# Layer 3's first keys and values, made in layer 2: a change to a four-layer Perceiver kernel

## The chip, the cores and the metric

The kernel runs on one core of a Trainium2 chip. The time is the device time of one execution in microseconds (us). TensorE (PE) multiplies, VectorE (DVE) and ScalarE (ACT) work on its results in PSUM, GpSimd (POOL) works in SBUF, and SyncE (SP) issues most DMAs. Each engine runs its own list of instructions strictly in the order in which the compiler put them.

## The reference, cut to what matters

Four layers run one after the other on `x`, 2 batches of 256 rows of 256 numbers, each with a cross-attention, a self-attention and a feed-forward part. Here only the end of layer 2 and the cross-attention of layer 3 matter:

```
x = x + L2_xattn(ctx, layernorm(x))           # a long convolution; the last stage before the change
x = x + L2_attn(layernorm(x), Wq, Wk, Wv)     # 16 heads of 16, rotary positions
x = x + L2_ffn(layernorm(x), ...)             # an attention again, then 8 experts, 2 per row
x = x + L3_xattn(layernorm(x), ctx, ctx, w_q, w_kv, w_concat)

def _L3_xattn_ref(q, kv, mem, w_q, w_kv, w_concat):
    c = concatenate([mem, kv], axis=1)        # the context twice: the softmax is that over it once
    qh = heads(q @ w_q)                       # 16 heads of 16
    kvp = c @ w_kv                            # ONE head of keys and values, shared by all 16
    k, v = kvp[..., :16], kvp[..., 16:]
    return concat(softmax(qh @ k.T / 4) @ v) @ w_concat
```

The context `ctx` is an input, 2 batches of 4096 rows. So the keys and values of layer 3 depend on no earlier layer: they can be made whenever the context is in SBUF.

## The kernel before, in words

All is float32. `perceiver` (L2466) calls one function per stage; `banks` gives out the 8 PSUM banks anew for each group of stages: in layer 2 (stage set "c") 3 banks "mm", 3 "tr", 2 "acc", in layer 3's cross-attention 4 "mm" and 4 "tr". SBUF is taken in pools that are stacked on one another; a pool that lies where an older one lay can be written only when the older one has been given free.

**Order.** Inside a block `in_order(...)` (L338) the instructions of the named engines stay as the code lists them. Elsewhere a planner in the compiler orders each engine's instructions: it goes through the program with its own estimates of time and gives a free engine the earliest listed instruction that it believes ready. Later instructions can so be put into an earlier gap, and once the order is made the engine keeps it.

**Layer 2, `l2_attn` (L1651) and the first half of `l2_ffn` (L1666).** Both project q, k and v (in `l2_attn` with a rotation in between, `rope_heads` L692, whose table `rope` is loaded by SP at L697) and call `self_attention` (L757). That runs steps k = 0 to 23 in order. `maxima(k)`, for k < 16, multiplies queries with keys (L785, into two "mm" banks) and DVE takes the row maximum of each bank (L791). `weights(k - 6)`, from k = 6 on, makes the scores again the other way round (L801, "tr" banks) and ACT takes the exponential (L808). `shift` (L815, L817) and `weigh` (L826) come in between. In k = 0 to 5, the *first maxima*, there are no weights, and the "tr" banks lie unused. Between the two attentions, at the *border*, lie the sum with `x` (L1661) and a norm (L386), both on DVE and ACT.

**Layer 3, `l3_xattn` (L2049).** `ctx_chunks` (L461) loads a batch's context in four chunks of 1 MB. `keys(b)` (L2068) makes a list of 12 steps of a batch: 8 times `key` (two matmuls of 512 columns, an ACT copy with bias, L2079), and two times `value` (8 matmuls 32 columns wide, L2088, ACT L2093) and `turned` (4 transposes L2098, ACT L2099). The queries are normed and projected (`proj_heads`). Then, in one block in order: two `key` steps of batch 0; a *ramp* of 18 turns, each with four matmuls for maxima (L2126), four DVE maxima (L2130) and one step of the list `made`; and a main loop of 8 groups of 16 turns, with the maxima of the next group, the weights (L2154, ACT L2158) and the sums (L2170) of this one, and a step of `made` while any is left. Of the 24 steps of both batches 2 stand ahead of the ramp, 18 in it, and 4 in the first turns of the main loop:

```
made.pop(0)()
made.pop(0)()
made += keys(1)
steps = maxima()
for _ in range(18):
    next(steps)
    next(steps)
    if made:
        made.pop(0)()
```

Weights that all stages load go through one ring of 4 buffers (`weight`, L314), issued by SP.

Of the kernel before, what the change touches and what calls it, by code (L numbers as in the profile page):

```python
# [268 lines left out]
class Perceiver:  # L269
# [486 lines left out]

    def self_attention(self, pool, qT, kT, v, scale):  # L757

# [8 lines left out]
        with ExitStack() as s:  # L767
# [65 lines left out]
            with self.in_order(e.PE, e.DVE, e.Activation):  # L833
                for k in range(16 + 6 + 2):
                    its = []
                    if k < 16:
                        its.append(maxima(k))
                    if 0 <= k - 6 < 16:
                        its.append(weights(k - 6))
                    then = None  # L840
                    if its:
                        self.steps_in_turn(*its)
                    if k % 4 == 0 and 4 <= k <= 16:
                        shift(k // 4 - 1)()
# [821 lines left out]
    def l2_ffn(self, x):  # L1666
        nc = self.nc
        T = NT * P
        with ExitStack() as s:
            keep = s.enter_context(self.tc.tile_pool(name="l2f_keep", bufs=1))  # L1670
# [77 lines left out]
            def unit(j):  # L1748
                def front():
                    gu, down = self.of_expert(pool, experts, j, ("l2f_gu", 1), ("l2f_down", 1))  # L1750
                    hT = p3.tile([P, KC, P], F32, name="rowsT", tag="rowsT")
                    if j < straight:
                        self.turn_chosen(pool, hT, h2, ats, along, j, "norm2")
                    else:
                        self.turn_rows(hT, rows, j, "norm2")
                    return expert(gu, down, hT, P, "e"), down
# [46 lines left out]
    def sort_rows(self, pool, chosen, n):  # L1803
# [52 lines left out]
    def send_rows(self, pool, x, slots, xs, first, n):  # L1856
# [3 lines left out]
        for t in range(NT):  # L1860
            for slot in slots:
# [7 lines left out]
                sent.append(i.ins.name)  # L1869
        rows = pool.tile([P, n, D], F32, name="rows")  # L1870
        for a, b in ((first, first + 2), (first + 2, n)):
            i = nc.gpsimd.dma_start(rows[:, a:b, :], xs[a * P : b * P].rearrange("(j p) d -> p j d", p=P))
            for name in sent:
# [43 lines left out]
    def ways_back(self, pool, ats, down, weights, first, n):  # L1917
# [5 lines left out]
        for j in range(first, n):  # L1923
# [123 lines left out]


    def l3_xattn(self, x, cpool):  # L2049

# [9 lines left out]
        with ExitStack() as s:  # L2060
            pool = s.enter_context(self.tc.tile_pool(name="l3x", bufs=1))
            kp = s.enter_context(self.tc.tile_pool(name="l3x_k", bufs=2))
            pt_pool = s.enter_context(self.tc.tile_pool(name="l3x_pt", bufs=16))
            wk, wv, wq = self.weight("l3x_wk"), self.weight("l3x_wv"), self.weight("l3x_wq")
            PAIRS = ((0, 1), (2, 3))
            kv = {}

            def keys(b):  # L2068

                cT = self.ctx_chunks(cpool, b, bufs=4)  # L2070
                kT = kp.tile([P, NK], F32, name="kT", tag="kT")
                v = kp.tile([P, 2, 4, 4, 32], F32, name="v", tag="v")
                kv[b] = kT, v.rearrange("p u g i d -> p (u g i) d")
                vTs = {}

                def key(j):
                    ps = self.bank([P, 512], "tr")
                    self.mm(ps, [(wk[:, k, :], cT[j // 2][:, k, ts(j % 2, 512)]) for k in range(KC)])
                    nc.scalar.activation(kT[:, ts(j, 512)], ps, AF.Identity, bias=self.col("lead"))  # L2079

                def value(u):


                    ps = self.bank([P, 512], "tr")
                    for k in range(KC):
                        for g in range(4):
                            j = 4 * u + g
                            nc.tensor.matmul(  # L2088
                                ps[ts(g, 32)], wv[:, k, :], cT[j // 2][:, k, ts(j % 2, 512)],
                                start=k == 0, stop=k == KC - 1,  # L2090
                            )
                    vTs[u] = pool.tile([P, 512], F32, name="vT", tag="vT")
                    nc.scalar.activation(vTs[u], ps, AF.Identity, bias=self.col("behind"))  # L2093

                def turned(u):
                    ps = self.bank([P, 4, P], "tr")
                    for i in range(4):
                        nc.tensor.transpose(ps[:, i, :], vTs[u][:, ts(i, P)], self.ident)  # L2098
                    nc.scalar.copy(  # L2099
                        v[:, u].rearrange("p g i d -> p i g d"), ps.rearrange("p i (g d) -> p i g d", d=32)  # L2100
                    )

                return [partial(key, j) for j in range(8)] + [partial(f, u) for u in range(2) for f in (value, turned)]

            made = keys(0)
            xnT = self.to_T(self.layernorm(x))
# [32 lines left out]
            def shifted(t, half, pad):  # L2139
                ps = self.bank([P, 2, P], "tr")  # L2140
                for c in range(2):
                    nc.tensor.transpose(ps[:, c, :], pad[:, c, :], self.ident)
                ready[t, half] = kp.tile([P, 2, P], F32, name="qm", tag="qm")
                nc.vector.tensor_add(ready[t, half], ps, qT[:, ts(half, 2), ts(t, P)])
# [227 lines left out]
    def l3_ffn(self, x):  # L2372
        nc = self.nc
        with self.tc.tile_pool(name="l3f", bufs=1) as pool, self.tc.tile_pool(name="l3f3", bufs=3) as p3:
# [34 lines left out]
            def unit(j):  # L2409
                def front():  # L2410
# [6 lines left out]
                    else:  # L2417
                        self.turn_rows(rT, rows, j)
                    hT = p3.tile([P, 8, P], F32, name="hT", tag="hT")
# [46 lines left out]
def perceiver(tc, dram, out, col_at, row_at, layers=LAYERS):  # L2466
    with ExitStack() as ctx:
        k = Perceiver(ctx, tc, dram, col_at, row_at)
        x = k.xp.tile([P, NT, D], F32, name="xres", tag="xres")
        tc.nc.sync.dma_start(x, dram["x"])  # L2470
        banks, tern, conv = ExitStack(), ExitStack(), ExitStack()
        k.tern = tern.enter_context(tc.tile_pool(name="l0f_w", bufs=1))
        for name in layers:
# [17 lines left out]
            elif name == "l2_attn":  # L2491
                conv.close()
                banks.close()
                k.banks(banks, "c", 3, 3, 2)
            elif name == "l3_xattn":

                banks.close()
                k.banks(banks, "l3x", 4, 4, 0)
            elif name == "l3_attn":
                banks.close()  # L2500
                k.banks(banks, "b", 3, 3, 2)
# [34 lines left out]
```

## Time and profile before

| | us |
|---|---|
| three runs | 2663.58, 2667.24, 2675.09 (median 2667.24) |
| profiled execution | 2663.32 |
| its span, first to last instruction | 2661.6 |
| end of the convolution stage, start of `l2_attn` | about 1630.3 |
| first maxima of `l2_attn` | 1656.2 to 1666.3 |
| border between the two attentions | 1706.6 to 1712.5 |
| first maxima of `l2_ffn` | 1734.0 to 1744 |
| context chunks of batch 0 issued | 1932.5 |
| ramp of layer 3 | 1949.7 to 2010.3 |
| main loop of layer 3 | from 2010.3 |

The page's first part gives the busy time of each engine and its share of the span. The second cuts the span into 40 equal slices of 66.5 us; each digit is a busy share in tenths, and the row PEclk is the share of its full clock that TensorE was granted. The timeline lists instructions in order of time: start, duration, engine, line, operation, result and operands, how many were merged (x4), and in brackets how long the engine had been idle and what ended that. One float32 matmul is two records of MATMUL in it, so x4 is two matmuls. Windows give, for stretches of time, the busy time of engines and the granted clock.

### The profile page before, as it was taken

What the parts mean: (1) busy time and instruction counts of PE and PEld (TensorE: products, weight loads), DVE (VectorE), ACT (ScalarE), POOL (GpSimd) and SP (SyncE); (2) the same over time, 40 slices, a digit from 0 to 9 for tenths busy, and PEclk for the clock granted to TensorE, in tenths of its full rate; (3) what the DMA queues carried; (4) which work ended last, traced back from release to release, by engine and by line L of the source; (5) the groups of instructions that cost most, each with busy time, mean ns of one, the idle gap of its engine ahead of it and who ended that gap; (6) DMA issues with size and microseconds to landing.
All of it is one profiled execution on the core that took longest, in us unless ns stands there. A gap on an engine that the chain in (4) does not pass through costs nothing. (4 is left out here: it accounts for less than half of the span.)

```text
span 2661.6 us, 45615 instructions
## 1 busy us (share of the span) xinstructions
PE 2493.7 (94%) x17709; PEld 1665.8 (63%) x17709; DVE 1727.2 (65%) x3195; ACT 1346.4 (51%) x2545; POOL 915.1 (34%) x861
## 2 busy tenths in 40 slices
PE   8986999999999999999799998889989999999889
PEld 6853566666666666666433555557835666554678
DVE  5566577777777777777669655454267788754542
ACT  3323666666666666666466322331116777784522
POOL 0520255655655655656459313001101222110010
PEclk9987999999999999999899998889999999999789
DMA  7210322222242222222300100017530000003656
GB/s 256 83 56 23 115 72 64 66 71 64 66 126 72 68 69 64 71 67 80 111 16 1 64 20 24 1 48 262 194 135 17 2 2 2 2 2 113 222 210 218
DMA packets 77111, 214.11 MB, mean 80 GB/s; under 512 B 6392, under 2 KB 21312, under 8 KB 66400
## 3 DMA queue, kind: packets, MB, share of 16 engines
q1 hardware_dynamic: 72128, 202.69, 22.9%
q0 software_dynamic: 1888, 5.90, 0.7%
q8 instruction: 139, 2.28, 0.4%
q10 hardware_dynamic: 2880, 2.62, 0.3%
q14 instruction: 76, 0.62, 0.1%
HBM read 190.48 MB, written 20.71 MB: 79 GB/s over the span
## 5 line engine op out<-in xcount | busy, mean ns | idle before, releaser
L1059 POOL TENSOR_TENSOR total<-total,S 128x512 f32<-128x512 f32 x434 | 542.2, 1280 | 304.7 <-ACT S L1048 304.7
L1048 ACT ACTIVATE S<-S 128x512 f32<-128x512 f32 x512 | 302.0, 625 | 209.5 <-DVE S L1045 209.3
L2130 DVE TENSOR_REDUCE mx<-ps_mm 128x1 f32<-128x512 f32 x512 | 318.0, 684 | 75.6 <-PE ps_tr L2154 58.9
L1034 DVE TENSOR_TENSOR most<-ps_mm,most 128x512 f32<-128x512 f32 x448 | 278.3, 684 | 119.2 <-ACT S L1031 119.2
L1031 ACT COPY S<-ps_mm 128x512 f32<-128x512 f32 x512 | 263.0, 599 | 116.7 <-PE ps_mm L1024 115.4
L1045 DVE TENSOR_TENSOR S<-S,ps_dec 128x512 f32<-128x512 f32 x512 | 317.6, 680 | 0.2 <-PE ps_dec L1103 0.2
L2158 ACT ACTIVATE PT<-ps_tr 128x512 f32<-128x512 f32 x476 | 246.9, 602 | 93.9 <-PE ps_tr L2154 89.0
L358 PEld LDWEIGHTS ps_tr<-w_l1x_wv,ctxT 128*128 128x128 f32 x2048 | 246.9, 192 | 52.9 <-issue 52.6
L1071 PE MATMUL acc<-S,v 128*64 128x256 f32 x2048 | 250.7, 387 | 7.8 <-ACT v L335 5.1
L1024 PE MATMUL ps_mm<-qT,kT 64*128 64x256 f32 x2048 | 257.1, 391 | 0.0
L358 PE MATMUL ps_tr<-ctxT,w_l1x_wk 128*128 128x512 f32 x512 | 251.8, 615 | 0.0
L2126 PE MATMUL ps_mm<-kT,qT 32*128 32x512 f32 x1024 | 250.6, 621 | 0.2 <-DVE mx L2130 0.2
L358 PE MATMUL ps_tr<-w_l1x_wv,ctxT 128*128 128x128 f32 x2048 | 250.1, 275 | 0.0
L2154 PE MATMUL ps_tr<-qm,kT 32*128 32x256 f32 x1904 | 239.7, 390 | 0.0
L1024 PEld LDWEIGHTS ps_mm<-qT,kT 64*128 64x128 f32 x2048 | 188.3, 187 | 38.9 <-DVE most L1034 3.8
L1071 PEld LDWEIGHTS acc<-S,v 128*64 128x64 f32 x2048 | 136.3, 137 | 104.8 <-ACT S L1031 38.8
L2154 PEld LDWEIGHTS ps_tr<-qm,kT 32*128 32x128 f32 x1904 | 170.3, 185 | 17.0 <-issue 6.5
L2179 POOL TENSOR_TENSOR sums<-sums,part 128x256 f32<-128x256 f32 x102 | 73.7, 722 | 269.2 <-ACT part L2178 269.2
L358 PEld LDWEIGHTS ps_tr<-ctxT,w_l1x_wk 128*128 128x128 f32 x512 | 89.7, 190 | 101.4 <-issue 99.9
L335 DVE COPY v<-ps_tr 128x512 f32<-128x512 f32 x120 | 82.9, 691 | 89.0 <-PE ps_tr L358 88.9
L2170 PE MATMUL ps_tr<-PT,v 128*32 128x256 f32 x2048 | 139.6, 385 | 0.0
L2126 PEld LDWEIGHTS ps_mm<-kT,qT 32*128 32x128 f32 x1024 | 85.5, 185 | 60.7 <-issue 48.4
(544 smaller groups left out, 3832.8 us busy)
## 6 DMA issues: line engine op xcount, KB each, us to landing
ctxT<-in_ctxT SPq DMA_DIRECT2D x144, 512.0 KB, 3.6
ctxT<-in_ctxT SPq DMA_DIRECT2D x16, 1024.0 KB, 7.5
w_l2f_gu<-in_l2f_gu SPq DMA_DIRECT2D x16, 1024.0 KB, 6.5
bd_dram<-bd SPq DMA_DIRECT2D x8, 1536.0 KB, 6.0
w_l3f_w<-in_l3f_w SPq DMA_DIRECT2D x11, 1028.0 KB, 8.2
w_l3f_w<-in_l3f_w SPq DMA_DIRECT2D x11, 1024.0 KB, 5.2
ctx<-in_ctx SPq DMA_DIRECT2D x8, 1024.0 KB, 4.9
w_l2f_down<-in_l2f_down SPq DMA_DIRECT2D x16, 512.0 KB, 4.1
```

The lines of the kernel that those rows point to most:

```text
L358: self.nc.tensor.matmul(out, lhsT, rhs, start=i == 0, stop=i == len(pairs) - 1)
L1024: nc.tensor.matmul(banks[hh, i][:, j, :], k[part, ts(2 * i + j, P)], q[u][part, :], start=True, stop=True)
L1031: nc.scalar.copy(t, ps)
L1034: nc.vector.tensor_tensor(m, ps, m, ALU.max)
L1045: nc.vector.tensor_tensor(t, t, spread[u][:, hh, :].unsqueeze(1).to_broadcast([P, 2, L]), ALU.add)
L1048: nc.scalar.activation(t, t, AF.Exp)
L1059: nc.gpsimd.tensor_add(tot, tot, t)
L1071: nc.tensor.matmul(av[u][part], vs[:, 2 * i + j, part], got[hh, i][:, j, :], start=g % 8 == 0 and i + j == 0, stop=g % 8 == 7 and i + j == 2,)
L2126: nc.tensor.matmul(ps, qT[rows, 2 * half + c, ts(t, P)], kT[rows, ts(j, 512)], start=True, stop=True,)
L2130: nc.vector.tensor_reduce(mx[:, c, r, j : j + 1], ps, AX.X, ALU.max)
L2154: nc.tensor.matmul(ps[:, i, :], kT[rows, ts(2 * u + i, P)], q[rows], start=True, stop=True)
L2158: nc.scalar.activation(pt, ps, AF.Exp, scale=0.25)
```

## The change

A function `l3_open`, called before `l2_attn`, opens a pool for keys, values and weights that lives through layer 3, and a pool for batch 0's context that lives until layer 2's second attention is done. It loads the two weights and the four context chunks and makes the 12 steps of batch 0. Four of them (`key` 0 to 3) run in `l2_attn`'s attention, one after each of the maxima k = 1 to 4; five (`key` 4 to 7, `value` 0) are listed at the border, outside any block in order; three (`turned` 0, `value` 1, `turned` 1) run after the maxima k = 1 to 3 of `l2_ffn`'s attention. In layer 3 only batch 1's 12 steps are left; they go into the first 12 turns of the ramp, and batch 1's chunks are loaded where batch 0's were. To make room, `sort_rows` uses the constant `ones`, `send_rows` keeps only the row tiles that are read from it, `other` shares two buffers with `places`, `qm` and `x1` move to other pools, and `l3x_wk`, `l3x_wv` leave the ring of weights.

```diff
-    def self_attention(self, pool, qT, kT, v, scale):
+    def self_attention(self, pool, qT, kT, v, scale, beside=()):
...
                     if its:
                         self.steps_in_turn(*its)
+                    if 0 < k <= len(beside):
+                        beside[k - 1]()
                     if k % 4 == 0 and 4 <= k <= 16:
...
-            z = self.self_attention(pool, qT, kT, v, 0.25)
+            z = self.self_attention(pool, qT, kT, v, 0.25, self.early[:4])
+            del self.early[:4]
             y = self.xp.tile([P, NT, D], F32, name="xres", tag="xres")
+            for step in self.early[:5]:
+                step()
+            del self.early[:5]
             for t in range(NT):
                 self.nc.vector.tensor_add(y[:, t, :], z[:, t, :], x[:, t, :])
...
-                z = self.self_attention(pool, qT, kT, v, 0.25)
+                z = self.self_attention(pool, qT, kT, v, 0.25, self.early)
                 zT = self.to_T(z, pool, "zT")
-                x1 = self.linear(zT, self.weight("l2f_wo"), x0, out=keep.tile([P, NT, D], F32, name="x1"))
+                x1 = self.linear(zT, self.weight("l2f_wo"), x0, out=self.kv.tile([P, NT, D], F32, name="x1"))
+            self.early_ctx.close()
...
-        before, ones = f("before", P), f("ones", P)
+        before, ones = f("before", P), self.ones
-        nc.gpsimd.memset(ones, 1.0)
...
-        rows = pool.tile([P, n, D], F32, name="rows")
+        rows = pool.tile([P, n - first, D], F32, name="rows")
...
-            other = pool.tile([P, NT * P], F32, name="other", tag="other")
+            other = pool.tile([P, NT * P], F32, name="other", tag="places", bufs=2)
...
+    def l3_open(self, ctx):
+        self.kv = ctx.enter_context(self.tc.tile_pool(name="l3x_kv", bufs=1))
+        self.l3w = []
+        for name in ("l3x_wk", "l3x_wv"):
+            self.l3w.append(self.kv.tile(list(self.dram[name].shape), F32, name=name))
+            self.nc.sync.dma_start(self.l3w[-1], self.dram[name])
+        self.early_ctx = ExitStack()
+        pool = self.early_ctx.enter_context(self.tc.tile_pool(name="l3x_ctx", bufs=1))
+        self.kv_first, self.early = self.l3_keys(self.kv, pool, self.ctx_chunks(pool, 0, bufs=4))
+
+    def l3_keys(self, kp, pool, cT):
...
+        kT = kp.tile([P, NK], F32, name="kT")
+        v = kp.tile([P, 2, 4, 4, 32], F32, name="v")
+        vTs = {}
+
+        def key(j):
+            ps = self.bank([P, 512], "tr")
+            self.mm(ps, [(wk[:, k, :], cT[j // 2][:, k, ts(j % 2, 512)]) for k in range(KC)])
+            nc.scalar.activation(kT[:, ts(j, 512)], ps, AF.Identity, bias=self.col("lead"))
+
+        def value(u):
...
+            vTs[u] = pool.tile([P, 512], F32, name="vT", tag="vT")
+            nc.scalar.activation(vTs[u], ps, AF.Identity, bias=self.col("behind"))
+
+        def turned(u):
...
+        steps = [partial(key, j) for j in range(8)] + [partial(f, u) for u in range(2) for f in (value, turned)]
+        return (kT, v.rearrange("p u g i d -> p (u g i) d")), steps
...
-            kv = {}
+            kv = {0: self.kv_first}
...
-            made = keys(0)
+            made = keys(1)
...
             with self.in_order(mybir.EngineType.PE, mybir.EngineType.DVE, mybir.EngineType.Activation):
-
-                made.pop(0)()
-                made.pop(0)()
-                made += keys(1)
                 steps = maxima()
...
                 k.banks(banks, "c", 3, 3, 2)
+                k.l3_open(first)
```

More of the change, by code (lines that the diff above doesn't have):

```diff
@@ L1669, in l2_ffn @@
         with ExitStack() as s:
-            keep = s.enter_context(self.tc.tile_pool(name="l2f_keep", bufs=1))
             with self.tc.tile_pool(name="l2f", bufs=1) as pool:
@@ L1754, in front @@
                     else:
-                        self.turn_rows(hT, rows, j, "norm2")
+                        self.turn_rows(hT, rows, j - straight, "norm2")
                     return expert(gu, down, hT, P, "e"), down
@@ L1869, in send_rows @@
                 sent.append(i.ins.name)
-        rows = pool.tile([P, n, D], F32, name="rows")
+        rows = pool.tile([P, n - first, D], F32, name="rows")
         for a, b in ((first, first + 2), (first + 2, n)):
-            i = nc.gpsimd.dma_start(rows[:, a:b, :], xs[a * P : b * P].rearrange("(j p) d -> p j d", p=P))
+            i = nc.gpsimd.dma_start(rows[:, a - first : b - first, :], xs[a * P : b * P].rearrange("(j p) d -> p j d", p=P))
             for name in sent:
@@ L2045, in top8 @@
         return top, atf
+    def l3_open(self, ctx):
[8 more added lines that the diff above has]
+    def l3_keys(self, kp, pool, cT):
+        nc = self.nc
+        wk, wv = self.l3w
+        kT = kp.tile([P, NK], F32, name="kT")
[6 more added lines that the diff above has]
+        def value(u):
+            ps = self.bank([P, 512], "tr")
+            for k in range(KC):
+                for g in range(4):
+                    j = 4 * u + g
+                    nc.tensor.matmul(
+                        ps[ts(g, 32)], wv[:, k, :], cT[j // 2][:, k, ts(j % 2, 512)],
+                        start=k == 0, stop=k == KC - 1,
+                    )
+            vTs[u] = pool.tile([P, 512], F32, name="vT", tag="vT")
+            nc.scalar.activation(vTs[u], ps, AF.Identity, bias=self.col("behind"))
+        def turned(u):
+            ps = self.bank([P, 4, P], "tr")
+            for i in range(4):
+                nc.tensor.transpose(ps[:, i, :], vTs[u][:, ts(i, P)], self.ident)
+            nc.scalar.copy(v[:, u].rearrange("p g i d -> p i g d"), ps.rearrange("p i (g d) -> p i g d", d=32))
+        steps = [partial(key, j) for j in range(8)] + [partial(f, u) for u in range(2) for f in (value, turned)]
+        return (kT, v.rearrange("p u g i d -> p (u g i) d")), steps
     def l3_xattn(self, x, cpool):
@@ L2061, in l3_xattn @@
             pool = s.enter_context(self.tc.tile_pool(name="l3x", bufs=1))
-            kp = s.enter_context(self.tc.tile_pool(name="l3x_k", bufs=2))
+            kp = s.enter_context(self.tc.tile_pool(name="l3x_k", bufs=1))
             pt_pool = s.enter_context(self.tc.tile_pool(name="l3x_pt", bufs=16))
-            wk, wv, wq = self.weight("l3x_wk"), self.weight("l3x_wv"), self.weight("l3x_wq")
+            wq = self.weight("l3x_wq")
             PAIRS = ((0, 1), (2, 3))
-            kv = {}
+            kv = {0: self.kv_first}
@@ L2068, in keys @@
             def keys(b):
                 cT = self.ctx_chunks(cpool, b, bufs=4)
[L2071 to L2103, printed above, removed]
@@ L2105, in l3_xattn @@
-            made = keys(0)
+                kv[b], steps = self.l3_keys(kp, pool, cT)
+                return steps
+            made = keys(1)
             xnT = self.to_T(self.layernorm(x))
@@ L2142, in shifted @@
                     nc.tensor.transpose(ps[:, c, :], pad[:, c, :], self.ident)
-                ready[t, half] = kp.tile([P, 2, P], F32, name="qm", tag="qm")
+                ready[t, half] = pool.tile([P, 2, P], F32, name="qm", tag="qm", bufs=2)
                 nc.vector.tensor_add(ready[t, half], ps, qT[:, ts(half, 2), ts(t, P)])
@@ L2417, in front @@
                     else:
-                        self.turn_rows(rT, rows, j)
+                        self.turn_rows(rT, rows, j - straight)
                     hT = p3.tile([P, 8, P], F32, name="hT", tag="hT")
@@ L2470, in perceiver @@
         tc.nc.sync.dma_start(x, dram["x"])
-        banks, tern, conv = ExitStack(), ExitStack(), ExitStack()
+        banks, tern, conv, first = ExitStack(), ExitStack(), ExitStack(), ExitStack()
         k.tern = tern.enter_context(tc.tile_pool(name="l0f_w", bufs=1))
@@ L2499, in perceiver @@
             elif name == "l3_attn":
+                first.close()
                 banks.close()
```

## The prediction, made before the changed kernel was run

> **What bounds the kernel now.** The page first:
>
> ```profile
> PE 2493.7 (94%) x17709; PEld 1665.8 (63%) x17709; DVE 1727.2 (65%) x3195; ACT 1346.4 (51%) x2545; POOL 915.1 (34%) x861
> PEclk9987999999999999999899998889999999999789
> ```
>
> TensorE is busy for 94% of the span, so moving its work pays only where it stands idle, or waits for DVE anyway, at the new place. The granted clock is at 8 tenths in the 25th to 27th digit (1597 to 1797 us), where layer 2's attentions lie: the place that receives the work. I then read the timeline of layer 3's ramp, where work is taken away:
>
> ```profile
> 1954.44 1.98 PE L358 MATMUL ps_tr<-ctxT,w_l3x_wk 128*128 128x512 f32 x4
> 1956.36 1.14 PE L2126 MATMUL ps_mm<-kT,qT 32*128 32x512 f32 x8
> 1957.43 1.98 PE L358 MATMUL ps_tr<-ctxT,w_l3x_wk 128*128 128x512 f32 x4
> ...
> 1961.11 1.99 PE L358 MATMUL ps_tr<-ctxT,w_l3x_wk 128*128 128x512 f32 x4
> ```
>
> Two turns, a `key` each, take 1961.11 - 1954.44 = 6.67 us: 3.33 per turn, set by PE (the chain of waits there alternates between L358 and L2126). With `value` and `turned` it is the same (1970.76 to 1977.36 to 1983.96). DVE follows with a gap per turn, and shows what it could do where PE is ahead:
>
> ```profile
> 1957.52 2.48 DVE L2130 TENSOR_REDUCE mx<-ps_mm 128x1 f32<-128x512 f32 x4 [1.19 <-PE ps_mm L2126]
> ...
> 1973.77 4.90 DVE L2130 TENSOR_REDUCE mx<-ps_mm 128x1 f32<-128x512 f32 x8 [0.44 <-PE ps_mm L2126]
> ```
>
> Eight maxima back to back last 4.90: a turn without a step costs DVE 2.45, and that is its floor.
>
> **What layer 3 gives back.** Ahead of the ramp, two `key` steps: the chain has their last six records from 1947.19 to the first maxima at 1949.77, 2.6 us; the first two ran at 1938.33 ahead of the queries' projection, which began its long run at 1940.24 and could, by the copy of xT (ACT, 1937.99 + 0.59), start at 1938.6 at the half clock still granted there; worked through, 0.8. Sum 3.4. In the ramp, 6 of 18 turns lose their step: 6 x (3.33 - 2.45) = 5.3. In the main loop the first four turns lose theirs: they begin at 2010.32 and end at 2026.76 (the starts of L2126), 16.44, where the next turn lasts 2.94; 16.44 - 4 x 2.94 = 4.7. One ACT table load of 1.28 at 2011.13 is in it; it came late because a key's copy stood ahead of it, so it goes too. **Sum 13.4 us**, and what is late next is DVE in the ramp, and the usual PE turn in the loop. Batch 1's chunks are not: they are issued where batch 0's were, at 1932.5; those landed after 4.7 to 12.1 us, by 1944.7, and batch 1's first key is due after 1946.
>
> **What layer 2 pays.** Each step is 1.92 on PE (1954.44 to 1956.36), `value` too, `turned` 0.6: 20.5 us for twelve. Their ACT copies (0.69, and 0.59) stand where ACT is nearly idle, 1.58 us busy in 10.1; the exception is the border, where one may hold up the norm's square root by up to 0.7.
>
> *Beside l2_attn's first maxima.* A turn there is two DVE maxima. The windows and the timeline:
>
> ```profile
> 1656.20:1666.30 10.10, 9.05 (x47) 5.71 (x46) 7.43 (x11) 1.58 (x2) 1.92 (x4) 0.71 0.00 0
> 1666.30:1690.00 23.70, 23.30 (x245) 15.23 (x245) 15.34 (x24) 11.42 (x21) 0.00 (x0) 0.84 0.01 2
> ```
>
> ```profile
> 1658.97 1.29 DVE L791 TENSOR_REDUCE mpad<-ps_mm 128x2 f32<-128x512 f32 x2 [0.20 <-PE ps_mm L785]
> 1660.47 1.44 DVE L791 TENSOR_REDUCE mpad<-ps_mm 128x2 f32<-128x512 f32 x2 [0.20 <-PE ps_mm L785]
> 1662.49 1.53 DVE L791 TENSOR_REDUCE mpad<-ps_mm 128x2 f32<-128x512 f32 x2 [0.58 <-PE ps_mm L785]
> ```
>
> The columns are window, length, then busy us of PE, PE's weight loads, DVE, ACT and POOL, the granted clock (0.71, 0.84), and DMA. Turns start 1.50 apart, DVE's pace, and from 1661 some 2.05 apart, because the clock is then 0.50 (2 us windows) until 1673. With a key, a turn is PE's: 0.85 for its maxima at full clock (four pairs of records 0.21 apart, as at 1680.4 to 1681.3) and 1.92, 2.8. Four such turns are 11.2 where four took 7.1; but if PE is kept busy as in layer 3's ramp (24.0 of 24.0 us, granted 1.00), the fall of the clock goes, which gives back 0.5 each in k = 5 and `shift` and 0.13 in some five turns of weights. 4.1 - 1.6 = **+2.5**, bounds -1 and +7.7 (four whole steps, nothing hidden).
>
> *At the border.* PE is idle there, then slow:
>
> ```profile
> 1712.46 2.19 PE L434 MATMUL ps_tr<-ident,xn 128*128 128x128 f32 x8 [5.85 <-DVE xn L404]
> 1714.86 8.88 PE L358 MATMUL ps_mm<-xT,w_l2f_wq 128*128 128x512 f32 x16 [0.21 <-DVE xT L438]
> 1723.58 7.03 PE L358 MATMUL ps_mm<-xT,w_l2f_wk 128*128 128x512 f32 x16
> ```
>
> The same 16 records take 8.88 after the gap and 7.03 later (clock 0.50 at 1708 to 1718). Five steps from 1706.6 on, back to back 8.9 (16 records of 0.43, a `value`, some 0.1 between), end at 1715.5, and the transposes that were at 1712.46 come 3.0 late; at full clock they save 1.1 and the projection 1.85. **+0.5** with some ACT delay; bounds -2 (the planner puts some into earlier gaps, such as 1647 to 1651, where PE waits for the rotation) and +4.
>
> *In l2_ffn.* `turned` twice fits into DVE's 1.50; `value` makes one turn 2.8. The half clock of 1739 to 1753 comes later or not at all. **0**, bounds -2 and +3.
>
> *The queue that is passed.* SP issues four chunks, as at 1932.52 (2.05 us for the four issues), when the convolution's memory is free, about 1630.3; the rotation's table, issued before at 1630.40, is listed behind them. They were 4 MB in 12.1 us, so the table lands near 1643.5 instead of 1633.3, and DVE's first rotation stood at 1640.25: **+3.2**, since DVE is busy without a break until the last one; bounds 0 (the planner puts the table first) and +5. A row for waiting in that queue: the 512 KB of `l3x_wq`, issued 0.4 us behind an expert's 1 MB, took 10.7 us, where `l3a_wr` took 3.4 alone. The two weights of the keys move past it too, and nobody waits for them.
>
> The rest is nothing, both ways under 1 us: the memset of `ones` (0.22 on an idle POOL), the smaller `rows`, `other` in a second buffer (four of 0.75 on DVE, whose users were long done), the shifted ring of weights (its loads get earlier), batch 1's four chunk issues at 1972.7 that go (in nobody's way).
>
> **The sum.** 2.5 + 0.5 + 0 + 3.2 = 6.2 paid, 13.4 given back: -7.2. The profiled execution was 2663.3, so 2656.1 by its own scale; the median shown is 3.9 higher. I forecast 2658, between the two.
>
> **Two rules of the Trainium skill against these rows.** "TensorE: Matmul & The Clock Gate", Part 1, section "What's actually happening", lets the clock fall to half after an idle window of some 3.4 us. The border's gap (5.85, then 0.50) agrees. The first maxima do not: their longest gap is 0.85 us, and the clock falls all the same; by the rule alone it is not lack of work that slows them, the 1.6 us would not come back, and the sum would be -5.6. "DMA: Bandwidth & Descriptors", section "Queues, rings and completion order", says that each DMA engine takes a ring's descriptors in order: that speaks against this change, as the small table is then bound to wait for the 4 MB; the 10.7 us agree, and my +3.2 stands; were it free to overtake, the sum would be -10.4.
>
> **Rivals.**
> 1. *Full cover*: the planner spreads the five loose steps over gaps of PE, the table is not late, the clock stays up. Then layer 2 pays 0: 2663.3 - 13.4 = 2649.9, lower still if half-clock stretches (some 25 us of busy PE) shrink. For it: PE idles 4 us in the rotation, 5.85 at the border. Against: the 1.92 of a key doesn't fit DVE's 0.2 to 0.7 of slack.
> 2. *Exposed*: PE's 20.5 us are paid in full beside the table's 3.2: 2663.3 - 13.4 + 23.7 = 2673.6. For it: 94% busy. Against: the border's idle time.
> 3. *Slower, by half speed*: the granted clock stays 0.50 where the moved steps run, in both first maxima and the border, so that a key is 3.44 + 0.2, its turn 5.3. Beside: 4 x 5.3 - 7.1 = 14.1; border 5 x 3.44 - 5.85 = 11.4; `l2_ffn` 3.5; table 3.2: +32 - 13.4 = 2682. It decides from the point where over half of the steps run at 0.50. Against: 1.00 in layer 3's ramp with the same mix.
> 4. *It does not give back what it says*: the ramp's freed turns stay at 3.33, for PE's own hand-over instead of its work. Then 5.3 are missing: 2663.
>
> **Chances.** Forecast 0.52; full cover 0.27; exposed 0.12; half speed 0.04; 4th 0.05. The range of 2646 to 2674 leaves out half speed and the outermost of full cover. Faster or slower counts from 0.5%, 13.3 us, about what a measurement of this kernel can tell from no change: below 2653.9 is most of full cover and a little of the forecast, 0.25; above 2680.6 half speed and a trace of the exposed case, 0.05; within 0.70.
>
> **What would show it.** L2126 starts as soon as the queries' projection ends; ramp turns of 2.45 from the 13th on; no L2088 in the main loop, whose first turns are 2.94; in layer 2 turns of 2.8 with clock 1.00 in the first maxima, no PE gap of 5.85 at the border, and the first L719 near 1643.5. I am wrong if PE, inside an order that the planner fixed, waits for a chunk that lands later than planned; if the maxima's clock stays at 0.50; or if the planner's order of the experts' stage, which the change does not touch, comes out differently.

## The result, and the profile after

The changed kernel takes as long as the kernel before. Measured beside each other, twice: first 2667.3 against 2666.2 us (ratio 1.0005, 95% interval 0.9995 to 1.0015), then 2670.7 against 2667.3 (1.0007, 0.9995 to 1.0019). The time lies in the predicted range, and I had given "within 0.5%" the largest chance, but the forecast's gain of 7.2 us is not there. The profiled execution spans 2665.4 us (before 2661.6). Its page, first the engines, then the clock:

```profile
PE 2495.4 (94%) x17708; PEld 1671.5 (63%) x17709; DVE 1722.2 (65%) x3195; ACT 1345.8 (50%) x2545; POOL 914.5 (34%) x859
...
PEclk9987999999999999999899998999898999999789
```

TensorE is busy for 1.7 us more, the same share; the clock's 26th and 27th digit (layer 2's attentions) have risen from 8 to 9, the 29th (the experts) and the 31st (1999 to 2066, the end of layer 3's ramp) have fallen from 9 to 8. The page can't say more, so I cut the execution at seven events that both kernels have and compared stretch by stretch. Single profiles differ by chance in places where the code is the same, so the table uses the profiles of programs that are the same in that stretch (six for layer 2: the changed kernel twice, and experiments that change something else).

| stretch | before, two profiles | changed program | difference | forecast |
|---|---|---|---|---|
| start to the projection of `l2_attn`'s queries and keys | 1635.8, 1635.8 | 1630.1 to 1634.2 | mean -3.1 | 0 |
| from there to its first maxima (rotation) | 20.47, 20.47 | 24.2 to 26.8 | mean +4.7 | +3.2 |
| to the end of its attention | 50.38, 50.36 | 52.6 to 55.8 | mean +4.2 | +2.5 |
| to the first maxima of `l2_ffn` (border, projections) | 27.37, 27.38 | 26.68, all | -0.7 | +0.5 |
| to the first expert's weights | 77.16, 77.16 | 74.1 to 83.4 | mean +2.0 | 0 |
| to layer 3's context issue, where no stall came (below) | 121.4 | 124.0, 124.2 | +2.7 | 0 |
| to the output projection of layer 3's cross-attention | 475.1, 475.2 | 466.7, 466.9, 467.8, 468.0 | mean -7.8 | -13.4 |

The sum is +2.0. Behind the last row 254.0 and 253.6 us are left in the kernel before and 252.2 to 254.4 in nine profiles of changed programs, 0.8 less in the mean; with it the sum is +1.2. Both are in keeping with the two ratios (+1.3 and +1.9 us). So the gain went three ways: layer 3 gives back 7.8 instead of 13.4; rotation, attention and border cost 8.2 where I had 6.2; and 2.7 are lost in the experts, where I had written "nothing".

**Layer 3.** DVE in the ramp of the changed kernel, from the 10th turn on (answers to the rows at 1957.52 and 1973.77):

```profile
1991.59 4.88 DVE L2152 TENSOR_REDUCE mx<-ps_mm 128x1 f32<-128x512 f32 x8 [1.13 <-PE ps_mm L2148]
1998.19 13.44 DVE L2152 TENSOR_REDUCE mx<-ps_mm 128x1 f32<-128x512 f32 x20 [1.73 <-PE ps_mm L2148]
2014.80 2.48 DVE L2152 TENSOR_REDUCE mx<-ps_mm 128x1 f32<-128x512 f32 x4 [1.51 <-PE ps_mm L2148]
2017.65 2.49 DVE L2152 TENSOR_REDUCE mx<-ps_mm 128x1 f32<-128x512 f32 x4 [0.37 <-PE ps_mm L2148]
```

The row of twenty maxima is the 12th turn, with the last short step behind it, and the first four of the six that lost theirs. They stand in one row, without a long gap, but take 13.44, not 5 x 2.45 = 12.3; the next two turns start 2.85 apart, and there are 3.2 us between the last of the twenty and the next, where the kernel before had 2.0. The windows (length, busy us of PE, weight loads, DVE, ACT, POOL, then the granted clock) say why:

```profile
1998.00:2002.00 4.00, 3.82 (x19) 1.96 (x15) 3.81 (x7) 1.87 (x2) 0.00 (x0) 1.00 0.01 2
2002.00:2022.00 20.00, 18.03 (x65) 11.14 (x66) 15.71 (x26) 0.82 (x2) 0.31 (x1) 0.52 0.00 0
2022.00:2026.00 4.00, 4.00 (x45) 2.98 (x40) 3.18 (x6) 3.04 (x7) 0.00 (x0) 0.84 0.00 0
```

Some 4 us after the last step the clock falls to half and stays there for 20 us, into the first turns of the main loop. In the kernel before it was 1.00 all that time: the steps that were taken away had kept it up (experiment 3 tests this). By the starts of DVE's maxima in six profiles without filling, the six freed turns of the ramp, the 13th to the 18th, take 19.5 to 19.9 us (before 21.5): the first 2.4 to 2.65, four some 2.85, and the 16th, which also hands the maxima of its group over to the weights (`mpad`), 5.7 to 6.1, where the kernel before has 4.46. The four freed turns of the main loop take 11.9 to 12.8 (before 16.4).

**Layer 2.** Beside the first maxima the keys run as I had them, a turn of 2.99 (I had 2.8), the first at half clock:

```profile
1657.84 3.61 PE L358 MATMUL ps_tr<-ctxT,l3x_wk 128*128 128x512 f32 x4
1661.38 1.15 PE L786 MATMUL ps_mm<-kT,qT 32*128 32x256 f32 x8
1662.46 1.98 PE L358 MATMUL ps_tr<-ctxT,l3x_wk 128*128 128x512 f32 x4
1664.37 1.13 PE L786 MATMUL ps_mm<-kT,qT 32*128 32x256 f32 x8
```

At the border the transposes of the norm follow the last step at once, at full clock (1.09, before 2.19), and the gap of 5.85 is gone:

```profile
1716.52 1.92 PE L2087 MATMUL ps_tr<-ctxT,l3x_wv 128*32 128x512 f32 x16
1718.38 1.09 PE L434 MATMUL ps_tr<-ident,xn 128*128 128x128 f32 x8
```

The turns and the border are thus nearly what my prediction said. The table's delay is there too, but dearer; SP issues it behind the four chunks:

```profile
1624.69 2.05 SPq L466 DMA_DIRECT2D ctxT<-in_ctxT  x4
1626.78 0.45 SPq L697 DMA_DIRECT2D rope<-in_rope  x1
```

It lands 11.2 us after its issue, at 1638.0 (before 2.9, at 1633.3). Yet DVE's first rotation comes later still: the planner has put three copies of products ahead of it, and the last of these waits for PE:

```profile
1640.97 0.42 DVE L332 COPY values<-ps_mm 128x256 f32<-128x256 f32 x1 [1.03 <-PE ps_mm L358]
1641.31 0.42 DVE L719 TENSOR_TENSOR rt<-tok,rope 128x256 f32<-128x256 f32 x1
```

In the six profiles with the late table the first rotation begins 0.1 to 3.3 us after the table has landed.

**The experts.** Here is the surprise, DVE's ways back (L1935 to L1938) and then the first projection that waits for them:

```profile
1866.45 0.75 DVE L1937 SCALAR_TENSOR_TENSOR other<-ats,down,by 128x512 f32<-128x512 f32 x1
1867.11 0.35 DVE L2032 TENSOR_SCALAR rowsT<-ps_tr,cols 128x128 f32<-128x128 f32 x1
```

```profile
1867.52 0.79 PE L358 MATMUL ps_mm<-rowsT,w_l2f_gu 128*128 128x128 f32 x2 [6.22 <-DVE rowsT L2032]
```

PE waits 6.22 us for the copy of the rows, where it waited 4.29 before. Eleven operations of the ways stand ahead of that copy, where eight stood.

### The profile page after: what moved, and what is told of

It reads as the page before. It is cut to its first block, busy times and chain, and to the rows that moved or that the text cites. A ratio compares the mean times of both kernels' runs of the same rounds, so it can differ in the third digit from the quotient of the medians.

```text
span 2665.4 us, 45605 instructions
## 1 busy us (share of the span) xinstructions
PE 2495.4 (94%) x17708; PEld 1671.5 (63%) x17709; DVE 1722.2 (65%) x3195; ACT 1345.8 (50%) x2545; POOL 914.5 (34%) x859
## 5 line engine op out<-in xcount | busy, mean ns | idle before, releaser
L358 PEld LDWEIGHTS ps_tr<-w_l1x_wv,ctxT 128*128 128x128 f32 x2048 | 247.0, 192 | 52.9 <-issue 52.6
L2148 PE MATMUL ps_mm<-kT,qT 32*128 32x512 f32 x1024 | 259.3, 639 | 1.1 <-DVE mx L2152 0.9
L2148 PEld LDWEIGHTS ps_mm<-kT,qT 32*128 32x128 f32 x1024 | 92.7, 189 | 62.9 <-issue 41.8
```

Of the source, the lines that this page charges most:

```text
L358: self.nc.tensor.matmul(out, lhsT, rhs, start=i == 0, stop=i == len(pairs) - 1)
L2148: nc.tensor.matmul(ps, qT[rows, 2 * half + c, ts(t, P)], kT[rows, ts(j, 512)], start=True, stop=True,)
```

## Experiments

Stretches are named as in the table. All edits are on the changed kernel unless said otherwise.

**1. `other` in one buffer again**

```diff
-other = pool.tile([P, NT * P], F32, name="other", tag="places", bufs=2)
+other = self.kv.tile([P, NT, D], F32, name="other", tag="x1")[:, 0:2, :].rearrange(...)
```

> The changed kernel, but `other` of the ways back has one buffer again (the memory of x1, which nobody reads by then). Theory A, the second buffer is what let the planner put eleven operations of the ways ahead of the rows' copy (1867.11) where eight stood before: PE's gap there falls from 6.22 to about 4.3 us, and the stretch from the first expert's issue to layer 3's context issue loses 2 to 2.5 us. Rival B, the gap is set by the transposes of positions on PE ahead of it: it stays at 6.2, whatever the order. The second stall of that stage (PE 2.43 idle at 1924.65, the ScalarE copy 5.75 late) has no tie to this edit: if it comes back at the same place, it belongs to the program (5 us in every run); if it is gone, it belonged to that one execution. Time: 2665 by A, 2667 by B, within the measurement's noise both.

Ratio 0.9990 (0.9980 to 1.0001). The order of before is back, eight operations and then the copy, and PE's wait with it:

```profile
1869.75 0.69 DVE L1938 TENSOR_TENSOR way<-way,other 128x512 f32<-128x512 f32 x1
1870.35 0.35 DVE L2032 TENSOR_SCALAR rowsT<-ps_tr,cols 128x128 f32<-128x128 f32 x1
```

```profile
1870.76 0.49 PE L358 MATMUL ps_mm<-rowsT,w_l2f_gu 128*128 128x128 f32 x2 [4.29 <-DVE rowsT L2032]
```

The stretch of the experts is 121.3, as before: theory A. In all profiles with two buffers the turn with the ways takes 14.5 us from one expert's first projection to the next, in all with one buffer 12.6.

**2. The rotation's table first**

```diff
 def l3_open(self, ctx):
+    self.tab = pool.tile([P, 2, 2, 8], F32, name="rope")   # pool: l3x_ctx, opened here
+    self.nc.sync.dma_start(self.tab, self.dram["rope"])
...
 def rope_heads(...):
-    tab = pool.tile([P, 2, 2, 8], F32, name="rope")
-    nc.sync.dma_start(tab, self.dram["rope"])
+    tab = self.tab          # in l2_attn
```

> The changed kernel, but the rotation's table is loaded ahead of layer 3's two weights and four chunks. Theory A, the table's place behind 4 MB is what made layer 2's rotation late: from the transposes of xn to the first maxima of l2_attn it takes 27.24 us in the changed kernel and 22.97 in the kernel before, and goes back to 23 here: 4.3 us less. Rival B, DVE or PE set that stretch, or the chunks' traffic slows the rest: less than 1 us is gained. Time: 2663 by A, 2667 by B.

Ratio 0.9977 (0.9966 to 0.9987). SP's queue is now:

```profile
1629.49 0.33 SPq L2065 DMA_DIRECT2D rope<-in_rope  x1
1629.86 2.04 SPq L466 DMA_DIRECT2D ctxT<-in_ctxT  x4
```

DVE's first rotation stands 4.0 us after the start of the projection (before 4.5, changed kernel 11.3), and the rotation takes 19.97, half a us less than in the kernel before. Theory A. The rest of `l2_attn` takes 52.65 here, and 50.96 and 52.78 in two later kernels with the table first, where those with the late table have 54.5 in the mean. That is not the table's doing: from the first maxima on, DVE's operations stand at the same distances in all these profiles, but for stretches of some 3.4 us at clock 0.50 that cost 1.6 each, one beside the first key (here, in the changed kernel's first profile and in experiment 1), up to three near the end. Without any (experiment 7) the attention takes 50.96. The moved steps alone thus cost +0.6 beside the maxima, and the late table 4.7. It is the dearest single cost found in this change, for an issue of 0.33 us. By the ratios 7 to 8 us are gained; what lies beyond the rotation's 5 is within their intervals.

**3. Filling the freed turns with a whole step**

```diff
 if made:
     made.pop(0)()
+else:
+    ps = self.bank([P, 512], "tr")
+    for c in range(2):
+        nc.tensor.matmul(ps, self.l3w[0][:, c, :], qT[:, c, :], start=True, stop=True)
```

> The changed kernel, with two matrix products of 128x512 whose result nobody reads in each of the six turns of layer 3's ramp that lost their step. Theory A, these turns cost more than 2.45 because TensorE, freed of the steps, lost its clock (0.50 from 2002 to 2023): filled, the clock stays at 1.00, five turns take 12.3 instead of 13.44, the first pad's gap 2.0 instead of 3.2, the first turns of the main loop 2.94; from the first maxima to the end of layer 3's cross-attention some 3.5 to 4 us are gained although PE does six more us of work. Rival B, the clock has no part, DVE sets the pace alone and PE's extra work stands in its way: no change, or up to 3 us slower. Rival C, the clock falls whatever PE does, as a budget: 0.50 comes at the same place and the products cost 6 us or more. Time: 2663.5 by A, 2667 to 2670 by B, 2673 by C.

Ratio 1.0004 (0.9990 to 1.0018). The clock is held:

```profile
1991.00:2012.00 21.00, 19.76 (x77) 7.51 (x74) 15.46 (x26) 1.96 (x3) 0.31 (x1) 1.00 0.00 0
```

So rival C is out, and the premise of A is shown: without the filling 0.52, with it 1.00. The freed turns of the main loop now take 11.6, all that I had forecast for them. In the ramp the gain that A expected did not come. I had taken two products for half a step; they are four records, 1.98 us, just what a key is, and the turns went back to 3.33. From the 12th turn to the 24th it takes 39.1 (before 43.8; changed kernel 38.1 and 36.8).

**4. Layer 3's side alone**

```diff
-self.kv_first, self.early = self.l3_keys(self.kv, pool, self.ctx_chunks(pool, 0, bufs=4))
+self.kv_first, self.early = self.l3_keys(self.kv, None, None)
+self.early = []
...
+nc.gpsimd.memset(self.kv_first[0], 0.01)    # in l2_ffn, and the same for the values
```

(with the single buffer of the first experiment)

> Layer 3's side alone: layer 2 makes no keys or values of the first batch and loads no chunks of context for them, so that its work is that of the kernel before; the keys and values of that batch are set to a constant on GpSimd after layer 2's attention, so the product's values are left out of the computation. `other` has a single buffer. My prediction's sum says that layer 3 gives back 13.4 us from the context issue to the end of its cross-attention, so 2653. Theory A, the freed turns lose TensorE's clock and the queries' projection starts late: 8.4 are given back, as in the profile of the changed kernel, so 2658. Rival B, the remaining loss in the changed kernel (12 us between the layers) is not layer 2's steps but chance of one execution: then this run is only about as fast as the changed kernel, 2663 to 2667.

Ratio 1.0002 (0.9992 to 1.0013). From the context issue to the output projection 7.1 are gained, so not the 13.4 of my sum. The total did not show them; the reason is my own edit, which the planner put elsewhere than I had written it:

```profile
1619.16 3.51 POOL L1688 MEMSET kT<- 128x4096 f32 x1
...
1620.49 2.20 DVE L366 TENSOR_SCALAR std<-bmv 128x2 f32<-128x2 f32 x1
```

The memset of the keys runs at the end of the convolution, and beside it a VectorE operation on two columns takes 2.20 us (0.17 in the kernel before), until the memset ends; the projection of `l2_attn` comes 33.9 us behind the first product with `w_l2x_w2a`, 4.7 more than in the kernel before (29.2).

**5. Filling the freed turns with half a step**

```diff
+    ps = self.bank([P, 512], "tr")
+    nc.tensor.matmul(ps, self.l3w[0][:, 0, :], qT[:, 0, :], start=True, stop=True)
```

> The changed kernel, with one matrix product of 128x512 (half of a step: two records, about 0.97 us) whose result nobody reads, in place of the step in each freed turn of layer 3's ramp. The heavy filling kept the clock at 1.00, but its two products are as long as a step, so that the turns stayed at 3.33. Theory A, a turn's own work is 3.33 - 1.92 = 1.41 on PE, and with 0.97 it stays below DVE's 2.45: turns of 2.45 at clock 1.00, main loop's first turns at 2.94; from the first maxima to the output projection layer 3 gains about 10 on the kernel before, where 4.4 to 6.3 were seen without filling and 3.7 with the heavy one; time 2663 (4 less than the changed kernel). Rival B, any work between the maxima opens DVE's gap of 0.5 to 1.2, through the buffers of PSUM: turns at 3.0 or more, no gain, 2667. Rival C, half a step does not keep the clock: 0.50 for some 20 us again, 2668 to 2670.

Ratio 0.9998 (0.9985 to 1.0011). The clock is 0.99 in the mean from 1990 to 2012, then 0.50 for some 3 us. That falls into the 16th turn, which takes 5.39; in experiments 7 and 10, with the same filling and clock 1.00, it takes 4.46, so that the clock alone cost 0.9 there. Two of the other turns together take 5.8: eight maxima in 4.88, and then a gap of 0.93, because PE has the product to do when DVE has emptied the buffers. From the 12th turn to the 24th 37.4 (36.5 in both later kernels with the same filling). Rival B: held clock or fallen clock, a freed turn costs 2.7 to 2.9, and 2.45 turn after turn is seen only in the few us before the clock falls.

**6. The kernel before, for a second profile**

> The kernel before, unchanged, for a second profile. Theory A, the stretches of layer 2 that differ by some us between kernels that have the same program there (76.0 to 80.8 us from the queries' weights to the router in l2_ffn) differ by the phase in which the clock falls, execution by execution: then this profile differs by several us from the first one there and in layer 1, and agrees within 0.5 us where the clock is 1.00 in both, such as layer 3's ramp and main loop. Rival B, they belong to the program: all stretches agree within 0.5 us with the first profile.

The time is 2669.6. It agrees with the first profile within 0.15 us in every stretch of the table but one (0.35 behind the last), the phase of the clock included: most of the expectation's theory A falls. The exception is the experts, 127.9 instead of 121.4. The reason is a stall in the 14th expert's turn, seen in the changed kernel too (1921 to 1925 there); `remote` means that the profile names nothing on this core that ended the wait:

```profile
1918.16 0.37 ACT L2030 COPY y_rows<-acc 128x256 f32<-128x256 f32 x1 [6.87 <-remote]
1918.22 0.69 DVE L1941 TENSOR_TENSOR xres<-acc,xres 128x512 f32<-128x512 f32 x1 [3.55 <-remote]
1918.58 1.13 PE L358 MATMUL acc<-y_rows,way 128*128 128x256 f32 x4 [3.55 <-ACT y_rows L2030]
```

That turn takes 8.4 us or 11.3 to 13.3, and nothing between; with what the slow clock adds after it, the stretch is 4 to 8 us longer. It came in 9 of 14 profiles, in one of the two of the kernel before and in both of the changed one, so that it needs no change to come. What sets it off stays open, but in these runs it goes with the chip, or the hour: none in experiments 1 to 4, all on one chip, and one in each of 5 to 12, on three others. For the first profiles of the two kernels the chip is not known. The kernel before has a median of 2661.8 on the first chip and of 2667.3 to 2668.3 on the others.

**7. The three mended together** (one buffer, table first, light filling)

> The changed kernel with the rotation's table first, a single buffer of `other`, and the light filling of layer 3's freed turns: the three costs that were found, taken away together. By addition: the table -7 (2654.4 against the changed kernel's 2663 or so on the same scale), the ways -2.5, the filling -4 (theory of the clock) or 0: 0.995 of the kernel before by the clock theory, 0.9965 without it. If the three overlap, or the moved steps themselves are what the change costs, it is no better than the table alone, 0.998.

Ratio 0.9957 (0.9942 to 0.9972): 2656.6 against 2668.3. It lies between the two cases expected, and its interval holds both. The stretches: rotation 20.47, attention 50.96, the ways' turn 12.6; from the 12th turn to the 24th 36.5.

**8. Filling the first maxima of layer 2, in the kernel before**

```diff
+if fill and k < 6:      # in l2_attn and l2_ffn
+    ps = self.bank([P, 256], "tr")
+    nc.tensor.matmul(ps, kT[:, 0, 0:P], kT[:, 0, 0:256], start=True, stop=True)
```

> The kernel before, with one product of 128x256 (about 0.48 us) whose result nobody reads after each of the first six turns of maxima in the attentions of l2_attn and l2_ffn. Theory A, the clock falls to 0.50 there because PE works only 0.85 of each 1.50 us: filled to 1.33, it stays at 1.00, turns stay at 1.50 instead of 2.05, and each of the two attentions gains 2 to 4 us: 0.998 of the kernel before. Rival B, the fall has been set off by the idle gaps ahead of the maxima (the rotation, the border) and comes some us late: it comes all the same, and PE's added work costs up to 3 us. Rival C, the attention does not need PE there: clock 1.00, but no gain.

Ratio 0.9970 (0.9954 to 0.9985): no useful work was added or moved, and the kernel is 6 us faster in its median, 8 by the ratio. The same window, first in the kernel before, then filled:

```profile
1661.00:1673.00 12.00, 12.00 (x65) 7.53 (x62) 7.54 (x12) 1.70 (x3) 0.00 (x0) 0.50 0.01 1
```

```profile
1661.00:1673.00 12.00, 11.44 (x105) 7.66 (x104) 9.83 (x16) 3.26 (x6) 0.00 (x0) 1.00 0.01 1
```

PE's records fill all of the first window and 11.44 us of the second; with the filling PE gets through 105 of them instead of 65, at clock 1.00 instead of 0.50. The added product holds PE for some 0.6 us of each turn:

```profile
1660.59 0.70 PE L845 MATMUL ps_tr<-kT 128*128 128x256 f32 x2
...
1662.49 0.70 PE L845 MATMUL ps_tr<-kT 128*128 128x256 f32 x2
```

Theory A, but smaller: the turns take 1.7 to 2.0, not 1.50; gained are 1.6 in `l2_attn`, 0.9 ahead of `l2_ffn`'s first maxima, 1.6 in its attention; 4 us, so that a part of the gain lies elsewhere or is noise.

**9. The filling cut small, one product of 128x128 after each maximum of the freed turns**

```diff
 nc.vector.tensor_reduce(mx[:, c, r, j : j + 1], ps, AX.X, ALU.max)
+if fill:
+    ps = self.bank([P, P], "tr")
+    nc.tensor.matmul(ps, self.l3w[0][:, 0, :], qT[:, 0, 0:P], start=True, stop=True)
```

> The changed kernel, with the filling of layer 3's freed turns cut small: one product of 128x128 whose result nobody reads after each single maximum, in place of one of 128x512 per turn. The light filling kept the clock at 1.00 for most of the stretch, but its turns took 2.9 (5.8 for two), as PE had a long product between two maxima when DVE had emptied the buffers. Theory A, the floor of 2.45 is DVE's and holds if PE is kept busy in pieces that fit between two maxima (0.6 us each): eight maxima follow each other in 4.9 without a gap, clock 1.00, and from the 12th turn to the 24th layer 3 takes 34 to 35.5 us (before 43.8; changed kernel 38.1; light filling 37.4 and 36.5). Rival B, any filling costs what the clock's fall costs: 36.5 to 38. Time: 2661 to 2664 by A, 2664 to 2667 by B, so the verdict is by the stretch and not by the total.

Ratio 1.0158 (1.0137 to 1.0178), some 42 us slower, far outside both theories.

```profile
1970.00:1999.00 29.00, 29.00 (x120) 9.92 (x118) 21.03 (x34) 6.18 (x9) 0.00 (x0) 1.00 0.01 5
2011.00:2047.00 36.00, 36.00 (x53) 12.98 (x52) 8.99 (x13) 0.00 (x0) 0.00 (x0) 0.50 0.00 0
```

```profile
2019.88 0.80 PE L2155 MATMUL ps_tr<-qT,l3x_wk 128*128 128x128 f32 x2
2020.60 2.07 PE L2148 MATMUL ps_mm<-kT,qT 32*128 32x512 f32 x2
```

A turn of four maxima takes 10.9. A maxima product uses 32 of the 128 rows (`32*128`), and two of a pair, on different rows, run over each other when they are issued back to back: eight records in 1.14. With a whole product between them each stands alone, 2.07 at half clock. And the clock is 0.50 although PE's records leave no idle time in the 36 us; in the 29 us of the first window, with steps between the maxima, they leave none either, and the clock is 1.00. So busy time by the records is not what keeps the clock up. More work on all 128 rows in the stretches where it stays up would explain it; no run varies that alone.

**10. The three mendings, and the first maxima filled where no step stands**

The filling of 8, after the mendings of 7, as `elif k < 6:` behind the moved steps, in `l0_attn` too.

> The three mendings together (table first, single buffer of `other`, light filling of layer 3's freed turns), and the filling of the first maxima with products of 128x256, in those of the first six turns of the attentions of l0_attn, l2_attn and l2_ffn that hold no moved step. If the two gains measured apart add up (0.9957 and 0.997), 0.993 of the kernel before; if the moved steps had already held up the clock in layer 2, and only l0_attn and two or three turns of each attention are left to fill, 0.994 to 0.9955.

Ratio 0.9943 (0.9929 to 0.9956): 2653.1 against 2667.7, the lowest ratio here; its interval doesn't decide between the two cases. By the stretches the second holds: `l2_attn`'s attention and the stretch of `l2_ffn`'s take 52.8 and 76.1 where experiment 7 has 51.0 and 75.5, and beside the first maxima the clock is 1.00 in both. The moved steps do already what the filling does in layer 2.

**11. and 12. Layer 3's side alone, and the changed kernel, once more**

> Layer 3's side alone once more, unchanged (the keys and values of the first batch are a constant, so they are left out of the computation): its profile had layer 3 7.1 us shorter, but its median was that of the kernel before. Theory A, the places where it lost (one VectorE operation of 2.20 us ahead of layer 2's first projection and the slow clock after it, 4.7; two falls of the clock in the attention of l2_ffn, 4.2) are chance of that execution: they are gone or elsewhere here, layer 3 is again 7 shorter, and the median of this group lies 3 to 7 us below the kernel before. Rival B, they belong to this program: the same stretches are longer by the same 4 to 5 us, and the median is again that of the kernel before.

Ratio 0.9991 (0.9982 to 1.0001). Rival B for the start: the memset of 3.51 us stands at the same place, VectorE's operation beside it takes 2.19, and the projection comes 4.3 late again; `l2_ffn`'s attention is longer again too, by 6.4 (4.2 in experiment 4). Layer 3's stretch is 8.8 shorter. Taking only the start's 4.7 and 4.3 off, the two runs say that layer 3's side alone is worth 4 to 7 us, a little less than the stretch (7.1 and 8.8).

> The changed kernel, unchanged, for a second profile and on the chip of the run beside it. Theory A, its ledger repeats where the clock's falls don't play: the rotation 4 to 6 us late, the ways' turn 14.5 instead of 12.6, layer 3 8 us shorter; the stall in the 14th expert's turn (12 instead of 8.4 us) comes or not, as in both profiles of the kernel before; layer 1 differs by some us. Time 1.000 to 1.002 of the kernel before. Rival B, the profile shown was an odd one, and the rotation or the ways take what they took in the kernel before: then it is 3 to 7 us faster than the kernel before.

Ratio 1.0007 (0.9995 to 1.0019). Theory A: rotation 24.4, the ways' turn 14.5, layer 3's stretch 467.8, the stall again.

## Why the prediction was right and wrong

- **Ahead of the ramp, 3.4 given back**: nearly right. From the context issue to the first maxima 2.0 to 3.2 are gained.
- **"In the ramp, 6 of 18 turns lose their step: 6 x (3.33 - 2.45) = 5.3"**: this is the step that failed. The six freed turns give back 1.5 to 2.0. I took the floor from rows that ran beside steps at clock 1.00, and asked what is late next as if the clock stayed; I had read that the first maxima of layer 2 run at 0.50 in just this mix, and did not carry it over. At half clock four of the six took 2.85, and the 16th, whose `mpad` my 2.45 left out, grew instead of shrinking. The clock's fall is shown (0.52 against 1.00 with filling); its price is measured alone only in one turn (0.9, experiment 5). The fillings tried brought little back, 19.5 to 22.0 for the six turns, as the filling itself opens DVE's gap.
- **"16.44 - 4 x 2.94 = 4.7"**: nearly right, 3.7 to 4.5, and 4.8 in the four profiles in which filling held the clock.
- **The ramp's turns 1 to 12**, which I took as unchanged: they hold the same kinds of steps in another order and take 0.2 more, and 1.9 more in five profiles, in which the second `value` turn ran at half clock.
- **Beside the first maxima, +2.5**: the mechanism was right: the clock stayed up beside the steps, but for the first key in some profiles. Without any fall it is +0.6; each 3.4 us at half clock adds 1.6, and with up to three of these the mean came to +4.2.
- **Border +0.5, `l2_ffn` 0**: the border gave back 0.7. In `l2_ffn` the mean of +2.0 comes from a spread of 9 us at the same code, as the clock falls at other moments; with so few profiles it does not differ from 0. (PE's idle time in the rotation, which I gave as 4 us, is 2.35 by its records.)
- **The table, +3.2**: the late table was right, the size too small, 4.7 in the rotation. I had the table land 7.7 us after the projection's start and the rotation begin with it; it landed 8.0 to 11.3 after, and the planner, which fixes the order by its own times, had put three copies ahead of the rotation, so that this began 10.5 to 11.3 after. The Trainium skill's "DMA: Bandwidth & Descriptors", section "Queues, rings and completion order", says that each DMA engine takes a ring's descriptors in order. The table's 11.2 us from issue to landing behind the chunks, 2.9 without them, agree.
- **"`other` in a second buffer (four of 0.75 on DVE, whose users were long done)"**: wrong, +2.7. I judged the memory and forgot the planner: a buffer more frees it to put three more operations ahead of the copy for which PE waits. My text had the case among what would prove me wrong, an order of the experts that comes out differently, but excluded the change as its cause.
- **Start to layer 2, 0**: -3.1 in the mean, though the operations are the same there. The clock falls at other moments on the way there: 1.6 us of the difference arise near 1605, where it is 0.57 from 1602 to 1606 in the kernel before and 1.00 in the changed kernel's second profile. Why the six profiles lie earlier than the two of before is open.

Put in, the terms make +2.0 where I had -7.2. The 9.2 between them are 5.6 from layer 3, 2.7 from the ways, 1.5 from the rotation, 1.7 from the attention behind it, 0.8 from border and `l2_ffn` together, less the 3.1 at the start. That the range held was the merit of its width, not of the sum, and the 3.1 at the start were luck.

## What to carry to other kernels

Before a step is taken off TensorE, ask whether it keeps the clock up for its neighbours: a stage that is left with thin products alone (here on 32 of the 128 rows) may lose in clock what it gains in work. When a transfer is moved ahead, first issue what is small and due sooner. And with a planner that orders by its own times, a buffer more or less is an edit of the order: compare the order on each engine, not only the memory.

## What the runs showed of the hardware

- The clock can stay at half without idle time in the records. The Trainium skill's "TensorE: Matmul & The Clock Gate", Part 1, section "What's actually happening", has a monitor of how busy TensorE is. Here 36.00 of 36.00 us were busy by the records, whose ends are modelled, and the clock was 0.50, with products on 32 rows and a small whole one of 0.7 us every 2.7 us (experiment 9); a whole product of 0.6 us in every 1.7 to 2.0 (experiment 8) kept 1.00. A monitor that counts the rows in use would fit; no run here shows that it does.
- A product on all rows between two on 32 rows takes away their overlap: 10.9 us at half clock for a turn that takes 2.85 without (experiment 9).
- A memset of 128x4096 on GpSimd (3.51 us) held up a VectorE operation beside it for 2 us: 2.20 and 2.19 instead of 0.17, ending with the memset both times (experiments 4 and 11).
- A stall of 3 to 4 us comes at the same place of a program in some executions and not in others (9 of 14): in none of four on one chip, in all eight on three others. All else agrees within 0.35 us a stretch between the two executions of the kernel before.
